# Cross-attention on one core: Wk loaded by row groups, two output tiles projected one batch later, the last tile's halves in two PSUM tiles

## The chip, the core and the metric

The kernel runs on 1 core of one Trainium2 chip. Its engines are TensorE (PE in the profile, with its weight loads as PEld), VectorE (DVE), ScalarE (ACT), GpSimd (POOL) and SyncE (SP), which does no arithmetic here and issues most of the DMA transfers. The metric is the device time of one execution in microseconds (us). Before the change the median of three runs was 953.03 us (952.38 to 954.02).

## What is computed

For each of 16 batches, with x of 100 rows by 640, a context of 718 rows by 384 (`enc`) and 4 more context rows (`ca`), in float32 throughout:

```python
query = x @ Wq;  keyt = enc @ Wk;  valt = enc @ Wv
hs = mha(query, keyt, valt)                       # 8 heads of 80
ca_q1 = einsum('btc,th->bch', ca, Wq_ca)[:, indices, :]
ca_hs1 = mha(ca_q1, x, x)
ca_q2 = ca_hs1 @ Wq;  ca_k2 = ca @ Wk_ca;  ca_v2 = ca @ Wv_ca
hs = hs + mha(ca_q2, ca_k2, ca_v2)
out = hs @ Wout + b_out + x
```

`mha` is softmax(q k^T / sqrt(80)) v for each head. The parts that matter for the change are the weight Wk, which is read once at the start, and the last line, the projection with Wout, whose rows are the 16 x 100 = 1600 rows of all batches.

## The kernel before

**Stages.** A startup part loads all weights and the first context, builds the values of batch 0 (`first_values`), folds Wk_ca with Wq (`k2_ps`, `m_ps`), transposes Wk on TensorE (`w_ps`, L1037) and makes the keys of batch 0 from it (`first_keys`, `kT_ps` L549), then the value projection of the 4 context rows (`va_ps`) and the queries of batches 0 and 1 (`q_ps` L525). After that a loop of 16 passes follows, one for each batch. In a pass PE makes scores (`s_ps` L604), small products of the second attention (`z_ps`, `y_ps`), the transpose of the previous batch's result (`hst_ps` L907), blocks of values and keys (`v_psA` to `v_psE` L425, `k_psA` to `k_psE` L456), the last chunk of the next batch's keys (`kT_ps`), perhaps a projection (`o_ps` L932), in odd passes the queries of the next two batches, and at last the attention sums (`a_ps` L1287). Up to the loop a scheduler orders the instructions of each engine; from `ctx.enter_context(tc.manual_schedule(...))` on they stand as written.

**Wk.** The host hands over Wk transposed: `wkt` has 640 rows (output columns of Wk) of 384. It is loaded into the space of `kT` as `wkt_sb`, five chunks of 128 partitions. `packed(w, c)` picks the rows of chunk c. For c below 4 these are 32 rows out of each of four groups of 160 rows (`RG` = 4, a group is two heads), so that group r lies on partitions 32r to 32r+31; chunk 4 holds the last 16 rows of each of the 8 heads. Each chunk is one transfer of 192 KB, issued by SP (L294), in program order. SP's queue has, in this order: pieces of the first context, `cat`, `wkca`, `wqt` (1600 KB), three more pieces of the context, `xT`, `ca`, the five pieces of `wkt`, five pieces of `wq`, `wvca`, and then `m_d`, which stores `m`. In the compiled program the transfers of SP and ACT take eight completion semaphores in turn, and a transfer waits, before it is issued, for the one that used its semaphore last.

The transposes of chunk c wait for chunk c's transfer alone; ACT copies each from PSUM into `wk_sb` or `wk4` (L1040), and `kT_ps` for a chunk needs the copy of this chunk only.

**The projection.** The 1600 rows are cut into tiles that don't follow the batches:

```python
OC = [(r, P) for r in range(0, B * S - P - 64, P)] + [(B * S - P - 64, 64), (B * S - P, P)]
```

These are eleven tiles of 128 rows, one of 64 and a last one of 128. A tile is projected when its last row's batch is done: `Last(b)` takes those whose end falls into batch b (`load`, L881), and pass b+1 calls its methods as `last`: `last.load()` loads the rows of x into `xn` on SP's queue and adds the bias on POOL (L892), `last.project()`, late in the pass, after the last keys and ahead of the queries and of `a_ps`, makes 10 matmul instructions into `o_ps` (two banks of 320 columns in one tile of two banks, `pair`), adds x on DVE (L951), and SP stores the rows (L952). Tiles end in batches 1, 2, 3, 5, 6, 7, 8, 10, 11, 12, 14, 14 and 15; none ends in 0, 4, 9 or 13. So tile 6 (rows 768 to 895, ends in batch 8) is projected in pass 9, tile 9 (rows 1152 to 1279, ends in batch 12) in pass 13. Passes 9 and 13 also have the queries; passes 10 and 14 have neither queries nor a projection. `hsT` and `xn` have two buffers each.

**The last tile.** Batch 15's tile is projected after the loop, in three calls of `project` for parts of its five chunks. Both halves (columns 0 to 319 and 320 to 639) lie in one two-bank tile; each half is added on DVE (L945) and stored by SP (L948) on its own. The pool `ps2`, which `pair` and `bank` draw from, has two tiles of two banks.

Of the kernel before, what the change touches and what calls it, by code (L numbers as in the profile page):

```python
# [10 lines left out]
ALU = mybir.AluOpType  # L11
# [3 lines left out]
B, S, H = 16, 100, 640  # L15
NH, D = 8, 80
CAD, T = 384, 4
SK = 722 - T
P = 128
HC = H // P  # L20
# [10 lines left out]


OC = [(r, P) for r in range(0, B * S - P - 64, P)] + [(B * S - P - 64, 64), (B * S - P, P)]
HT = NH * T

QC = [(0, 64), (64, S)]
# [10 lines left out]
for h in range(NH):  # L47
    lo = h * D
    while lo < (h + 1) * D:
        c = lo // P  # L50
        hi = min((h + 1) * D, (c + 1) * P)
        PIECES.append((h, c, lo - h * D, lo - c * P, hi - lo))
        lo = hi
# [15 lines left out]
RG = 4  # L69


def packed(w, c):

    if c < 4:
        lo = (c // 2) * D + 32 * (c % 2)
        return w.rearrange("(r k) n -> r k n", r=RG)[:, lo : lo + 32]
    return w.rearrange("(h k) n -> h k n", h=NH)[:, 64:]

# [44 lines left out]
def kernel(  # L125
# [18 lines left out]
    nc = tc.nc  # L144
# [14 lines left out]
    def pair(name):  # L159
        tile = ps2.tile([P, 2, 512], F32, tag="ps2", name=name)  # L160
        return tile

    def bank(name):
        return pair(name)[:, 0]
# [18 lines left out]
    def scores_tile(name):  # L183
        return main.tile([P, 2, ROWS], F32, tag="st", name=name, bufs=NP)

    def hs_tile(name):
        return main.tile([P, H], F32, tag="hs", name=name)

    def hsT_tile(name):
        return main.tile([P, HC, P], F32, tag="hsT", name=name, bufs=2)  # L190

    def xn_tile(name):
        return main.tile([P, H], F32, tag="xn", name=name, bufs=2)

    def vb_tile(name):
        return main.tile([P, T, H], F32, tag="vb", name=name)
# [46 lines left out]
    def in_order(dma):  # L243
        tc.keep_in_program_order(dma)
# [27 lines left out]
    for g in range(2):  # L272
        for c in range(CC):
            nc.scalar.dma_start(
                out=wv_sb[:, 2 * c + g],
                in_=wv[c * P : (c + 1) * P, g * (H // 2) : (g + 1) * (H // 2)],
# [9 lines left out]
    wkt_sb = kT.rearrange("p c u k -> p c (u k)")  # L286
# [3 lines left out]
    in_order(nc.sync.dma_start(out=xT, in_=xt[0:2].rearrange("b p c s -> p b c s")))  # L290
    ca_0 = small.tile([S, T, S], F32, tag="ca", name="ca_0", bufs=2)
    in_order(nc.sync.dma_start(out=ca_0, in_=cas[0].unsqueeze(0).to_broadcast([S, T, S])))
    for c in range(HC):
        in_order(nc.sync.dma_start(out=wkt_sb[:, c, :CAD], in_=packed(wkt, c)))  # L294
    halves = [t[:, u] for t in [scores_tile(f"wq_{i}") for i in range(NP)] for u in range(2)]
    room = halves.pop()
    wq_in = [t[:, :H] for t in halves]
# [16 lines left out]

    m2 = const.tile([P, HC, NG, HT], F32, name="m2")
    nc.gpsimd.memset(m2, 0.0)
    for h, c, r, s, k in PIECES:
        nc.gpsimd.dma_start(
            out=m2[s : s + k, c, GROUPS[c][1].index(-1), h * T : (h + 1) * T],
            in_=wqcat[h * D + r : h * D + r + k, :],  # L320
# [4 lines left out]
    for c in range(HC):  # L325
        first = c * P - HEADS[c][0] * D
        nc.gpsimd.affine_select(
            out=hmask[:, c], in_=hmask[:, c], compare_op=ALU.is_ge, fill=0.0,
# [3 lines left out]
            out=hmask[:, c], in_=hmask[:, c], compare_op=ALU.is_ge, fill=0.0,  # L332
# [6 lines left out]

    m_sb = [t[:, : B * HT] for t in (hs_tile("m_0"), xn_tile("m_1"), xn_tile("m_2"))]  # L340
    m_sb += [
        hsT_tile(f"m_{c}").rearrange("p c s -> p (c s)")[:, : B * HT] for c in range(3, HC)
    ]
    m_d = dram.tile([HC, P, B * HT], F32, name="m_d")

# [7 lines left out]
    for j in range(2):  # L353
        y = const.tile([S, NH, HT + 1], F32, name=f"y_{j}")
        nc.gpsimd.memset(y[:, :, HT:], 1.0)
        ys.append(y)
# [352 lines left out]
    class Second:  # L709
# [98 lines left out]
        def load(self):  # L808
            b = self.b
            self.vb = vb = vb_tile(f"vb_{b}")  # L810
            nc.gpsimd.dma_start(
                out=vb[:S],
                in_=va_d[b * T : (b + 1) * T, :].unsqueeze(0).to_broadcast([S, T, H]),
            )
# [58 lines left out]
    class Last:  # L873
# [7 lines left out]
        def load(self):  # L881

            self.xn = {}
            for r, (lo, n) in enumerate(OC):
                if not self.b * S < lo + n <= (self.b + 1) * S:
                    continue
                xn = self.xn[r] = spare[1] if r == len(OC) - 1 else xn_tile(f"xn_{r}")
                rows = x.rearrange("b s n -> (b s) n")[lo : lo + n]
                for at, cols in self.parts(n):
                    to = xn[at : at + n, : cols.stop - cols.start]  # L890
                    nc.sync.dma_start(out=to, in_=rows[:, cols])
                    nc.gpsimd.tensor_tensor(to, to, bias[at : at + n, cols], ALU.add)  # L892
# [7 lines left out]
        def transpose(self, chunks=[(0, HC)]):  # L900
# [4 lines left out]
            for c0, c1 in chunks:  # L905
                for c in range(c0, c1):
                    nc.tensor.transpose(  # L907
                        t_v[:, c], hs[:S, c * P : (c + 1) * P], ident[:S, :S]
                    )
                for r, (lo, n) in enumerate(OC):  # L910
                    first, end = max(lo, b * S), min(lo + n, (b + 1) * S)
                    if first >= end:
                        continue
                    if r not in hsTs:
                        hsTs[r] = (
                            spare[0].rearrange("p (c s) -> p c s", c=HC)
                            if r == len(OC) - 1
                            else hsT_tile(f"hsT_{r}")
# [6 lines left out]
        def project(self, chunks=range(HC)):  # L925
            for r, xn in self.xn.items():
                lo, n = OC[r]
                if chunks[0] == 0:
                    self.o_ps = pair(f"o_ps_{r}")
                o_ps = self.o_ps  # L930
                for c, k in [(c, k) for k in range(2) for c in chunks]:
                    nc.tensor.matmul(  # L932
                        o_ps[:n, k, : H // 2],
                        hsTs[r][:, c, :n],
                        wout_sb[:, c, k * (H // 2) : (k + 1) * (H // 2)],
                        start=(c == 0),
                        stop=(c == HC - 1),
                    )
                if chunks[-1] < HC - 1:
                    continue  # L940
                o_v = out.rearrange("b s n -> (b s) n")[lo : lo + n]
                if self.split:
                    for k in range(2):
                        cols = slice(k * (H // 2), (k + 1) * (H // 2))
                        nc.vector.tensor_tensor(  # L945
                            xn[:n, cols], o_ps[:n, k, : H // 2], xn[:n, cols], ALU.add
                        )
                        nc.sync.dma_start(out=o_v[:, cols], in_=xn[:n, cols])  # L948
                    continue
                both = xn[:n].rearrange("p (k d) -> p k d", k=2)  # L950
                nc.vector.tensor_tensor(both, o_ps[:n, :, : H // 2], both, ALU.add)  # L951
                nc.sync.dma_start(out=o_v, in_=xn[:n])  # L952

        def project_few(self, r):
            lo, n = OC[r]
            xn = self.xn.pop(r)
            o_ps = psumk(f"o_ps_{r}")
            for c in range(HC):
                for at, cols in self.parts(n):
                    nc.tensor.matmul(  # L960
                        o_ps[at : at + n, : H // 2],
                        hsTs[r][:, c, :n],
                        wout_sb[:, c, cols],
                        start=(c == 0),
                        stop=(c == HC - 1),
                    )
            nc.vector.tensor_tensor(
                xn[:, : H // 2], o_ps[:, : H // 2], xn[:, : H // 2], ALU.add
            )
            o_v = out.rearrange("b s n -> (b s) n")[lo : lo + n]  # L970
            for at, cols in self.parts(n):
                nc.sync.dma_start(out=o_v[:, cols], in_=xn[at : at + n, : H // 2])
# [26 lines left out]
    for n, heads in enumerate(HEADS):  # L999
        cols = len(heads) * B * T  # L1000
# [77 lines left out]
    for n in range(2):  # L1078
        nc.scalar.dma_start(
            out=va_d[:, n * (H // 2) : (n + 1) * (H // 2)],  # L1080
            in_=va[n * B * T : (n + 1) * B * T],
# [20 lines left out]
    for b in range(B):  # L1102
        p = b // 2
# [174 lines left out]
        for g in range(2):  # L1278
# [20 lines left out]
            cols = slice(4 * g * D, 4 * (g + 1) * D)  # L1299
# [65 lines left out]
```

## Time and profile before

| what | value |
|---|---|
| median of three runs | 953.03 us (952.38 to 954.02) |
| the profiled execution | 953.95 us |
| its span on the core | 952.2 us |
| mean granted clock of TensorE | 0.998 |
| DVE, ACT, POOL busy | 677.3, 362.1, 628.4 us |
| HBM traffic | 64 GB/s over the span |

The span runs from the first to the last instruction that the hardware profiler has on the core; 1.75 us of the execution lie outside it. "Busy" is the time in which an engine works on instructions; idle time before a group is put down to what released it. Of the largest groups on PE, `s_ps` has 3072 matmul rows of 32x100 and 768 of 32x200, `a_ps` 3072 rows, and `o_ps` 130 matmul instructions that show as 260 rows, because each float32 matmul stands as two rows in the trace. POOL's sums of context blocks (`enc`, L491) make up 101.6 + 32.8 us, in 180 instructions.

The startup up to the first scores takes 65.7 us. Lines of the stages below are given as L numbers of the kernel before.

### The profile page before, as it was taken

The numbers are of one execution on the slowest core, as the hardware profiler recorded it, in microseconds if no ns is written. First come the engines' busy times: TensorE is split into PE (matmuls) and PEld (weight loads), VectorE is DVE, ScalarE is ACT, GpSimd is POOL, SyncE is SP. The second block draws the span as 40 slices with busy tenths as digits, with TensorE's granted clock in tenths as the row PEclk, the third lists the DMA queues.
The fourth block names the chain that finished last, engine by engine and source line by source line (L and its number), as shares of the span: only waits on it lengthen the run. The fifth ranks groups of instructions, "written<-read, shape, count | busy, mean of one in ns | idle before, by whom it ended". The sixth has DMA issues, their size and how long they took to land.

```text
span 952.2 us, 25609 instructions
## 1 busy us (share of the span) xinstructions
PE 939.3 (99%) x11215; PEld 799.2 (84%) x11215; DVE 677.3 (71%) x1083; ACT 362.1 (38%) x598; POOL 628.4 (66%) x570
## 2 busy tenths in 40 slices
PE   9899999999999999999999999999999999999998
PEld 6898879879898888978789787898889888898866
DVE  1659795786928879496964959569793786928883
ACT  1234442444314344343524335243431444314341
POOL 4639979576846677496773958638694576845723
PEclk9999999999999999999999999999999999999999
DMA  8743014031130402204050040401204031120100
GB/s 253 221 142 98 3 44 136 2 95 37 50 102 1 115 2 80 59 1 129 1 149 3 6 125 1 136 3 46 71 17 135 2 100 31 47 84 1 59 8 29
DMA packets 45255, 62.48 MB, mean 66 GB/s; under 512 B 13336, under 2 KB 37208, under 8 KB 43544
## 3 DMA queue, kind: packets, MB, share of 16 engines
q1 hardware_dynamic: 41608, 42.97, 15.2%
q0 software_dynamic: 2512, 16.72, 6.0%
q8 instruction: 88, 1.44, 0.6%
q10 hardware_dynamic: 1024, 1.15, 0.4%
q14 instruction: 23, 0.19, 0.1%
HBM read 55.26 MB, written 5.57 MB: 64 GB/s over the span
## 4 chain that ended last, share of the span: by engine, by line
PE 94%; DMA 3%; DVE 1%; ACT 0%; issue 0%; SPq 0%; ACTq 0%; DVEq 0%
PE s_ps L604 12%; PE a_ps L1287 12%; PE v_psA L425 10%; PE v_psB L425 8%; PE k_psA L456 7%; PE kT_ps L549 7%; PE q_ps L525 7%; PE o_ps L932 7%; PE k_psB L456 6%; PE v_psC L425 3%; PE k_psC L456 3%; PE v_psD L425 2%; PE v_psE L425 2%; PE y_ps L730 2%; DMA kT<-in_wkt 1%; PE k_psE L456 1%
## 5 line engine op out<-in xcount | busy, mean ns | idle before, releaser
L765 POOL TENSOR_TENSOR e<-ca,g 100x800 f32<-100x800 f32 x64 | 99.4, 1564 | 135.0 <-DVE most L1136 120.9
L854 POOL TENSOR_TENSOR hs<-vb,p 100x640 f32<-100x640 f32 x64 | 105.0, 1650 | 45.9 <-DVE p L840 37.9
L861 POOL TENSOR_TENSOR hs<-hs,hs 100x640 f32<-100x640 f32 x48 | 115.1, 2397 | 3.8
L1287 PEld LDWEIGHTS a_ps<-vs,st 120*64 120x64 f32 (+3 forms) x3072 | 109.1, 125 | 7.3 <-issue 5.9
L1287 PE MATMUL a_ps<-vs,st 120*64 120x81 f32 (+3 forms) x3072 | 112.3, 234 | 1.6 <-ACT st L1132 1.0
L425 PE MATMUL v_psA<-wv_sb,enc 128*120 128x320 f32 x360 | 112.0, 434 | 0.0
L1124 DVE TENSOR_TENSOR st<-st,over 120x1600 f32<-120x1600 f32 x48 | 108.2, 2255 | 0.0
L491 POOL TENSOR_TENSOR enc<-enc 128x240 f32<-128x240 f32 x135 | 101.6, 766 | 7.1
L604 PE MATMUL s_ps<-qp,kT 32*120 32x100 f32 x3072 | 98.0, 263 | 0.8 <-issue 0.8
L621 ACT COPY st<-s_ps 120x800 f32<-120x800 f32 x64 | 49.7, 829 | 126.2 <-PE s_ps L604 126.2
L604 PEld LDWEIGHTS s_ps<-qp,kT 32*120 32x120 f32 x3072 | 95.1, 179 | 2.6 <-issue 1.2
L772 POOL TENSOR_TENSOR e<-e,e 100x800 f32<-100x800 f32 x48 | 92.2, 1922 | 3.8
L425 PE MATMUL v_psB<-wv_sb,enc 128*120 128x320 f32 x300 | 93.1, 433 | 0.0
L456 PE MATMUL k_psA<-enc,wk_sb 128*128 128x240 f32 x360 | 87.6, 366 | 0.0
L1298 DVE RECIPROCAL rs<-a_ps 100x4 f32<-100x4 f32 x32 | 5.8, 182 | 113.8 <-PE a_ps L1287 113.8
L425 PEld LDWEIGHTS v_psA<-wv_sb,enc 128*120 128x120 f32 x360 | 64.5, 183 | 23.0 <-issue 0.5
L1136 DVE TENSOR_TENSOR most<-most,st 120x800 f32<-120x800 f32 x64 | 66.4, 1038 | 22.8 <-ACT st L615 21.8
L1132 ACT ACTIVATE st<-st 120x1600 f32<-120x1600 f32 x48 | 73.8, 1538 | 23.1 <-DVE st L1124 23.1
L456 PEld LDWEIGHTS k_psA<-enc,wk_sb 128*128 128x128 f32 x360 | 68.3, 190 | 16.7
L491 POOL TENSOR_TENSOR enc<-enc,rest 128x240 f32<-128x240 f32 x45 | 32.8, 729 | 73.0 <-DMA rest<-in_enct 24.9
L425 PEld LDWEIGHTS v_psB<-wv_sb,enc 128*120 128x120 f32 x300 | 54.8, 183 | 22.1 <-DVE vs L396 0.4
L456 PE MATMUL k_psB<-enc,wk_sb 128*128 128x240 f32 x300 | 73.1, 366 | 0.0
(137 smaller groups left out, 1769.4 us busy)
## 6 DMA issues: line engine op xcount, KB each, us to landing
vb<-va_d POOLq DMA_DIRECT2D x16, 1000.0 KB, 7.8
enc<-in_enct SPq DMA_DIRECT2D x30, 240.0 KB
enc<-in_enct SPq DMA_DIRECT2D x15, 360.0 KB
xT<-in_xt SPq DMA_DIRECT2D x8, 500.0 KB
rest<-in_enct SPq DMA_DIRECT2D x31, 120.0 KB
xn<-in_x SPq DMA_DIRECT2D x11, 320.0 KB
out<-xn SPq DMA_DIRECT2D x11, 320.0 KB
ca<-in_cas SPq DMA_DIRECT2D x16, 156.2 KB
```

Source lines behind the costliest of these rows:

```text
L425: nc.tensor.matmul(at[0][j][:KN, : H // 2], a_form(self.enc, f)[:, j * KN : (j + 1) * KN], wv_sb[:, W_AT[f]], start=first, stop=last, skip ...
L456: nc.tensor.matmul(at[:, i * KT : (i + 1) * KT], wk_sb[:, W_AT[f], i], a_form(self.enc, f), start=(first and i == 0), stop=last, skip_grou ...
L491: nc.gpsimd.tensor_tensor(out, left, right, op)
L525: nc.tensor.matmul(q_ps[:, : 2 * S].rearrange("p (j s) -> p j s", j=2), wq_sb[:, c, n * P : (n + 1) * P], xT[:, :, c, :], start=(c == 0), ...
L604: nc.tensor.matmul(s_ps[r][:n, 256 * a + lo : 256 * a + hi], kT[rows, c, u, j * KN : (j + 1) * KN], rhs, start=(a == 0 and c == 0), stop=( ...
L765: first = nc.gpsimd.tensor_tensor(to, self.ca[:, t, :].unsqueeze(1).to_broadcast([S, NH, S]), g[:, :, t].unsqueeze(2).to_broadcast([S, NH, ...
L772: nc.gpsimd.tensor_tensor(e, e, to, ALU.add)
L854: first = nc.gpsimd.tensor_tensor(to, vb[:S, t, :].rearrange("p (h d) -> p h d", h=NH), p2[:, :, t].unsqueeze(2).to_broadcast([S, NH, D]), ...
L861: nc.gpsimd.tensor_tensor(sums, sums, to, ALU.add)
L1124: return nc.vector.tensor_tensor(st[i], st[i], top.over[:KN].unsqueeze(1).to_broadcast([KN, 2, ROWS]), ALU.subtract,)
L1132: nc.scalar.activation(st[i], st[i], AF.Exp, scale=SCALE)
L1287: nc.tensor.matmul(a_v[lo:hi, h % 4], st[i // 2][: KEYS[i], i % 2, h * S + lo : h * S + hi], block(i, h // 4)[: KEYS[i], h % 4], start=(i ...
```

## The change

Three edits. Wk's chunks 0 to 3 are loaded in eight transfers instead of four, each for one row group r and one of its two heads u: 32 partitions, two chunks at a time, 96 KB. Chunk 4 is loaded as before. Tiles are assigned to passes by `O_AFTER` in place of their end: a tile that ends in an even batch b goes to batch b+1 when no tile ends there. That holds for b = 8 and b = 12, so tile 6 is projected in pass 10 and tile 9 in pass 14; their loads and bias adds move along. The last tile's halves lie in two tiles of PSUM, each the first bank of a pair.

```diff
+ENDS = [(lo + n - 1) // S for lo, n in OC]
+O_AFTER = [b + 1 if b % 2 == 0 and b + 1 not in ENDS else b for b in ENDS]
...
-def packed(w, c):
-
-    if c < 4:
-        lo = (c // 2) * D + 32 * (c % 2)
-        return w.rearrange("(r k) n -> r k n", r=RG)[:, lo : lo + 32]
-    return w.rearrange("(h k) n -> h k n", h=NH)[:, 64:]
+def load_packed(load, to, w):
+
+    rows = w.rearrange("(r u k) n -> r u k n", r=RG, u=2)
+    for r, u in [(r, u) for r in range(RG) for u in range(2)]:
+        load(
+            out=to[32 * r : 32 * r + 32, 2 * u : 2 * u + 2],
+            in_=rows[r, u, :64].rearrange("(j p) n -> p j n", j=2),
+        )
+    load(out=to[:, 4], in_=w.rearrange("(h k) n -> h k n", h=NH)[:, 64:])
...
-    for c in range(HC):
-        in_order(nc.sync.dma_start(out=wkt_sb[:, c, :CAD], in_=packed(wkt, c)))
+    load_packed(
+        lambda **ends: in_order(nc.sync.dma_start(**ends)), wkt_sb[:, :, :CAD], wkt
+    )
...
             for r, (lo, n) in enumerate(OC):
-                if not self.b * S < lo + n <= (self.b + 1) * S:
+                if self.b != O_AFTER[r]:
                     continue
...
-                if chunks[0] == 0:
-                    self.o_ps = pair(f"o_ps_{r}")
+                if chunks[0] == 0 and self.split:
+                    self.o_ps = [bank(f"o_ps_{r}_{k}") for k in range(2)]
+                elif chunks[0] == 0:
+                    self.o_both = pair(f"o_ps_{r}")
+                    self.o_ps = [self.o_both[:, k] for k in range(2)]
...
-                        o_ps[:n, k, : H // 2],
+                        o_ps[k][:n, : H // 2],
...
-                            xn[:n, cols], o_ps[:n, k, : H // 2], xn[:n, cols], ALU.add
+                            xn[:n, cols], o_ps[k][:n, : H // 2], xn[:n, cols], ALU.add
...
-                nc.vector.tensor_tensor(both, o_ps[:n, :, : H // 2], both, ALU.add)
+                nc.vector.tensor_tensor(
+                    both, self.o_both[:n, :, : H // 2], both, ALU.add
+                )
```

Nothing else differs. In the compiled program the instructions of ACT keep their order; on PE and DVE the projections of the two tiles stand one pass later, on POOL and SP their bias adds, loads and stores. SP issues four transfers more. In the transposes of Wk on PE, those of chunks 0 and 1 now wait for the four transfers with u = 0, those of chunks 2 and 3 for the four with u = 1.

## The prediction

> **What bounds the kernel now.** I read the page first: the engine totals, then the 40 slices, then the chain that ended last.
>
> ```profile
> PE 939.3 (99%) x11215; PEld 799.2 (84%) x11215; DVE 677.3 (71%) x1083; ACT 362.1 (38%) x598; POOL 628.4 (66%) x570
> ...
> PE   9899999999999999999999999999999999999998
> ...
> PE 94%; DMA 3%; DVE 1%; ACT 0%; issue 0%; SPq 0%; ACTq 0%; DVEq 0%
> ```
>
> PE is busy for 939.3 of 952.2 us. No step of the change takes a matmul away, so all it can win is idle PE, slow PE and the tail behind the last matmul. The only slices under 9 are the second and the last. The list of PE's waits names the largest single one: the transposes of Wk, for the transfers into kT, 2.6 us, once. A table in steps of 1 us around it shows what that wait costs (columns: window, length, busy time and count of PE, PEld, DVE, ACT, POOL, granted PE clock, share of the 16 DMA engines, GB/s):
>
> ```profile
> 23.00:24.00 1.00, 1.00 (x9) 1.00 (x8) 0.53 (x3) 0.00 (x0) 0.00 (x0) 1.00 0.27 100
> ...
> 31.00:32.00 1.00, 0.82 (x6) 0.58 (x6) 0.26 (x1) 0.47 (x2) 0.75 (x3) 1.00 0.83 224
> 32.00:33.00 1.00, 0.00 (x0) 0.00 (x0) 0.00 (x0) 0.67 (x3) 1.00 (x1) 1.00 0.73 138
> 33.00:34.00 1.00, 0.00 (x0) 0.00 (x0) 0.00 (x0) 0.00 (x0) 1.00 (x2) 1.00 0.79 201
> 34.00:35.00 1.00, 0.60 (x3) 0.63 (x4) 0.00 (x0) 0.00 (x0) 0.92 (x2) 0.53 1.08 376
> 35.00:36.00 1.00, 1.00 (x7) 0.80 (x6) 0.00 (x0) 0.26 (x1) 1.00 (x1) 0.50 1.02 368
> 36.00:37.00 1.00, 1.00 (x5) 0.94 (x5) 0.75 (x2) 0.94 (x3) 0.92 (x2) 0.50 1.02 393
> 37.00:38.00 1.00, 1.00 (x6) 0.90 (x5) 1.00 (x2) 0.14 (x1) 1.00 (x1) 0.77 1.04 383
> ```
>
> See two things: PE stands still from 31.82 to 34.40, and then runs 3.5 us at half clock. And at 23 us, with Wk the only load under way, 0.27 of 16 engines, about four, move 100 GB/s; at 14 to 16 us the same table gives 406.
>
> **Part 1, the load of Wk.** SP issues its transfers in order, and each waits for the one eight places earlier in the program. So later issues show when pieces of Wk landed (timeline of SP, and of PE):
>
> ```profile
> 28.72 0.33 SPq L299 DMA_DIRECT2D wq<-in_wq  x1
> 31.47 0.38 SPq L300 DMA_DIRECT2D wvca<-in_wvca  x1
> 34.35 0.33 SPq L1026 DMA_DIRECT2D m_d<-m  x1
> ...
> 34.40 2.01 PE L1037 MATMUL w_ps<-ident,kT 128*128 128x128 f32 x8 [2.58 <-DMA kT<-in_wkt]
> ```
>
> These wait for the second, third and fourth piece: 192 KB every 2.8 us. PE starts 0.05 us after the fourth; the fifth frees SP at 35.68.
>
> Why four engines? [...] Old pieces are 4x32x384 into 128x384: 4 engines, as the row at 23 us has it. New ones are 32x2x384 on both sides: 16. [...]
>
> When do the new pieces land? The first goes at 12.24. The second waits for wkca (the present second piece, 14.98, has that wait), the third to sixth for wqt and enc (from 20.13, about 0.5 us apart). The seventh and eighth wait for xT and ca; the present second and third wq transfers, which do so too, are out by 24.34 and 25.59. The ninth waits for the first. All are issued by about 26.1, and 960 KB at 300 to 400 GB/s is 2.5 to 3.3 us, which runs from about 23. Last landing: about 28, at the latest 26.1 + 2.8 = 28.9. The transposes begin at 30.19. So **the wait goes**, although a chunk is now whole only with its fourth row group, the seventh piece for chunks 0 and 1.
>
> What is late next? The first six transposes end at 31.82 as before (m and y_ps precede them). Two of chunk 3 follow, to 32.05. Chunk 2 takes the PSUM bank of y_ps, which ACT copies out until 31.91 + 0.38 = 32.29. Seven more at 0.11 to 0.15 us end at 33.1 to 33.4. kT_ps then starts at 33.2 instead of 36.42: **3.2 us**. Its first eight matmuls take 2.14 us now (36.42 to 38.56), later ones 0.2025 each, so 1.62: another **0.5 us** of clock. [...] The row shows half clock after 2.58 us, and the mean clock of 0.998 is 1.7 us lost in the whole run, all here. I take 3.7, ends 2.4 (a new wait) and 4.3 (2.58 + 1.7).
>
> Is it given back? wq and wvca leave SP earlier than now. DVE's copies of wq (36.25 to 45.2) start near 31.7, beside POOL's e products, and q_ps needs them only at 57.1 - 3.7. The POOL sums for batch 1 start at 62.78, when enc lands; that load waits for PE's va_ps, so it moves along, but wout and xT, held by POOL, don't, and may delay it by 1 us. POOL idles 1.18 us after the sums, so I cost that at nothing; without this cover it costs up to 1 us. The stalls of batches 0 and 1 (a_ps 1.0, hst_ps 1.2) hang on DVE and ACT, which hang on PE: they move along and stay.
>
> **Part 2, two tiles one batch later.** Tile 6 moves from pass 9 to pass 10, tile 9 from 13 to 14: per tile 20 o_ps rows (5.4 us of PE), one DVE add (0.82), one POOL bias add (about 0.8 to 1.6), one load and one store on SP. PE's sum stays. Passes 9 and 13 keep q_ps (8.5 us) between kT_ps and a_ps, as pass 5 has it now; passes 10 and 14 have nothing there now. The chain behind pass 10:
>
> ```profile
> 665.84 6.90 PE a_ps L1287 x191
> 672.73 0.40 PE s_ps L604 x8
> 673.13 0.80 issue
> 673.93 7.29 PE s_ps L604 x224
> ...
> 681.53 0.18 issue
> ...
> 683.84 1.10 PE v_psA L425 x4
> ```
>
> From s_ps to v_psA is 11.11 us; nearly every other pass has 9.52 (624.33 to 633.85). **1.6 us** are lost, and PE waits for nothing that the profile names. My reading is late instructions: a_ps and s_ps are hundreds of short ones, and here they come without a pause while DMA is 0.91 to 1.02 busy (664 to 672). Passes with 5.4 us of o_ps ahead of the same burst don't show it. With o_ps in pass 10, a_ps starts when the burst is over. I take 1.6; ends 1.8 (pass 14 loses 0.2) and a loss of 0.6 (a gap like the one of 0.57 in batch 1 appears elsewhere).
>
> The rest is covered. In pass 10 the bias add stands on POOL before the products that wait 2.2 us for DVE. The DVE add comes while PE runs 6.9 us of a_ps. Of SP: loads of tiles 10 and 11 and of spare now queue behind the store of tile 9. In the present clock pass 14's o_ps would end at 894.3 (894.31 is a_ps's start now; pass 13 gives back what pass 14 takes), so the store goes near 895.5 in place of 838.46. Tile 11 also needs it landed; loads then land by about 901, POOL's bias adds (3.3 us for these tiles now) end by 905, and the DVE add that needs them comes at 916.02. Slack 11 us; cost nothing, one for one beyond it.
>
> **Part 3, the last tile's halves.** Now both halves share a tile, and DVE waits for all of it:
>
> ```profile
> 943.96 4.35 PE o_ps L932 x16
> ...
> 948.33 0.49 DVE spare L945
> ...
> 948.90 0.84 SPq L948 DMA_DIRECT2D out<-spare  x2
> ```
>
> Five of these eight matmul instructions (two rows each, 0.54 us) finish half 0, at 946.7; its add and store lie beside the last three. Half 1 is added at 948.33 and not 0.4 later, and its store, second of 0.84 us, is issued 0.4 to 0.5 earlier with no other on the queue: **0.5 us**, ends 0.2 and 0.9. The second tile takes the pair that tile 10's add left at 935.5, long before.
>
> **The sum.** 3.7 + 1.6 + 0.5 = 5.8. The profiled execution took 953.95 (span 952.2, 1.75 around it): 948.15. It stands 0.9 above the median of 953.03, inside the runs' 952.38 to 954.02; from the median the sum gives 947.2. I put the forecast between, at **947.6**.
>
> **Rivals.**
> - The gap of pass 10 is bad luck of one place, and stays or moves. For: the trace has it once. Against: eleven covered passes are free of it. Startup and tail alone: 4.2, so 949.2. Chance 0.2.
> - Another wait takes the place: enc's load behind wout, then POOL's 11.2 us of sums in batch 0, eats 2.5 us of the startup's gain. Against: the POOL slack above. 950.1. Chance 0.1.
> - The change doesn't do what it says: Wk lands as late as now, because SP's waits and not engines hold it. Then parts 2 and 3 alone, 951.5. Against: only four engines move at 23 us. Chance 0.05.
> - Slower: the engines of a piece are counted from its dimension of 2, not of 32. By the same rule two engines then carry 256 rows each where four carry 128 each in 13.57 us (20.69 to 34.26 in the chain): 27 us, landing at 48, and kT_ps 13 us late; 953.5 + 13 - 2.1, about 964. It decides once the last piece lands over 2.1 us later than the present 35.6. Against: the program issues 32x2x384 with 32 outermost. Chance 0.04.
>
> The forecast has 0.61. A measurement of this kernel tells about 0.2%, 1.9 us, from no change. Faster by more: forecast, the first two rivals and part of the third, 0.91; same 0.05; slower 0.04. The range adds up low ends (4.3 + 1.8 + 0.9 from the median, and runs that differ by 0.5) and goes up to the second rival: 945.6 to 950.5.
>
> **What would show it.** Right: no wait of w_ps for kT, kT_ps near 33.2, clock 1.00 from 30 to 40 us, DMA share near 1 at 24 us; s_ps to v_psA 9.52 us in batch 11; the first spare add near the end of half 0. Wrong: clock below 1 there, "issue" gaps at other passes, a wait of POOL's enc sums that grows, or o_ps of pass 14 followed by a late L967 add.

## The result, and the profile after

The changed kernel takes **946.35 us** in the median of six runs (945.60 to 946.49); the kernel before took 953.28 us beside it (six runs, 952.38 to 954.02). The ratio is 0.9924, with a 95% interval of 0.9915 to 0.9934, so 6.9 us less (6.3 to 8.1). The profiled execution took 945.6 us, its span 943.9.

The page of the changed kernel: engine totals, PE's 40 slices, and the shares of the chain that ended last.

```profile
PE 935.4 (99%) x11215; PEld 796.8 (84%) x11215; DVE 680.7 (72%) x1083; ACT 361.8 (38%) x598; POOL 626.0 (66%) x570
...
PE   9999999999999999999999999999999999999998
...
PE 95%; DVE 3%; ACT 1%; DMA 0%; issue 0%; POOL 0%; ACTq 0%; DVEq 0%
```

PE has the same 11215 rows, 3.9 us less of busy time, and no slice under 9 at the start any more. DMA has 0% of the chain in place of 3%.

The startup, in windows of 1 us (columns as in the prediction: length, busy time and count of PE, PEld, DVE, ACT, POOL, granted clock of PE, share of the 16 DMA engines, GB/s):

```profile
22.00:23.00 1.00, 1.00 (x10) 1.00 (x9) 0.21 (x2) 0.00 (x0) 0.00 (x0) 1.00 1.01 195
23.00:24.00 1.00, 1.00 (x10) 1.00 (x9) 0.62 (x1) 0.00 (x0) 0.29 (x1) 1.00 0.65 139
24.00:25.00 1.00, 1.00 (x10) 1.00 (x10) 0.69 (x1) 0.00 (x0) 0.00 (x0) 1.00 0.23 63
...
31.00:32.00 1.00, 1.00 (x10) 0.97 (x8) 1.00 (x1) 1.00 (x3) 1.00 (x1) 1.00 0.93 317
32.00:33.00 1.00, 1.00 (x7) 0.94 (x6) 1.00 (x2) 0.50 (x2) 1.00 (x2) 1.00 1.02 369
33.00:34.00 1.00, 1.00 (x7) 0.94 (x6) 1.00 (x3) 0.00 (x0) 0.92 (x2) 1.00 1.01 320
34.00:35.00 1.00, 1.00 (x7) 0.94 (x6) 1.00 (x1) 0.56 (x1) 1.00 (x1) 1.00 0.97 369
```

From 31 us on PE is busy and at full clock, where it stood still and then ran at half clock before. But at 24 us the DMA share is 0.23 and not near 1: the engines are full at 22 us and three quarters idle two microseconds later. The timeline of SP's queue and of PE, in the same kernel:

```profile
12.14 13.89 SPq L302 DMA_DIRECT2D kT<-in_wkt  x9
26.08 2.35 SPq L308 DMA_DIRECT2D wq<-in_wq  x5
...
29.83 1.82 PE L1051 MATMUL w_ps<-ident,kT 128*128 128x128 f32 x13
31.50 1.38 PE L558 MATMUL kT_ps<-enc,wk_sb 128*128 128x240 f32 x6
```

Nine transfers of Wk are issued by 26.03, and the transposes of Wk don't wait for them. Wk's rows can be told from all others in the traces' DMA records, as packets of 1536 bytes, 640 of them. In the changed kernel 358 have started by 24 us, at up to 118 in 1 us (181 GB/s). The last three transfers are issued from 23.81 on, and the last row is in at 28.72. In the kernel before, 127 have started by 24 us and the last row is in at 34.81. From its traces:

```profile
23.67 5.37 SPq L299 DMA_DIRECT2D wq<-in_wq  x5
...
28.00:29.00 1.00, 1.00 (x10) 1.00 (x9) 0.69 (x1) 0.00 (x0) 0.03 (x1) 1.00 1.09 274
```

Here wq shares the engines with Wk. Its first rows move at 25.05, when 210 rows of Wk have started, and in each microsecond from 26 to 32 only 33 to 48 rows of Wk start, where it was 65 at 23 us. In both kernels wq stands behind Wk in SP's queue, but it takes SP longer to get nine transfers out than five (13.89 us against 11.39). In the changed kernel wq is issued from 26.08 and moves from 27.40, when 533 rows of Wk have started. So the change did two things at once: it gave Wk's pieces more engines, and it put wq off.

The chain behind pass 10 (start, length, what):

```profile
654.26 5.38 PE o_ps L944 x20
659.64 6.90 PE a_ps L1301 x191
666.54 7.28 PE s_ps L613 x240
673.82 0.68 PE z_ps L801 x56
...
676.07 1.10 PE v_psA L434 x4
```

`o_ps` of tile 6 now stands ahead of `a_ps`. No piece is called "issue", and from `s_ps` to `v_psA` it is 9.53 us, against 11.11.

The tail, in the timeline of all engines:

```profile
935.77 4.50 PE L944 MATMUL o_ps<-wout_sb,spare 128*128 128x320 f32 x16
...
938.69 0.49 DVE L957 TENSOR_TENSOR spare<-o_ps,spare 128x320 f32<-128x320 f32 x1 [3.29 <-PE o_ps L944]
939.26 1.90 SPq L960 DMA_DIRECT2D out<-spare  x2
940.31 0.49 DVE L957 TENSOR_TENSOR spare<-o_ps,spare 128x320 f32<-128x320 f32 x1 [1.12 <-PE o_ps L944]
```

The first add lies beside `o_ps`, and only the second is left behind its end at 940.27.

Where the 8.3 us between the two profiled spans lie, by the same marks in both traces:

| stretch | before | after | difference |
|---|---|---|---|
| start to the first `k_ps` | 20.22 | 18.83 | -1.39 |
| `k_ps` to `kT_ps` | 16.20 | 12.67 | -3.53 |
| `kT_ps` to `q_ps` | 20.61 | 20.09 | -0.52 |
| behind pass 10, `s_ps` to `v_psA` | 11.11 | 9.53 | -1.58 |
| pauses in batch 1 and pass 12 | | | -1.00 |
| end of the last `o_ps` to the end | 3.90 | 3.63 | -0.28 |

The first row is not of the change. `k_ps` starts before anything that the change touches is needed, and in the eleven profiles here, all with the same early loads, it starts at 18.3 to 20.2. Nor are the pauses of the fifth row shown to be: in batch 1 a kernel with all three parts has one of 0.30 us (the last experiment), and the kernel with the tiles alone has none. Without these two rows the pair differs by 5.9 us.

### The profile page after: what moved, and what is told of

Same layout as the page of the kernel before. It is cut to its first block, busy times and chain, and to the rows that moved or that the text cites. A ratio compares the mean times of both kernels' runs of the same rounds, so it can differ in the third digit from the quotient of the medians.

```text
span 943.9 us, 25613 instructions
## 1 busy us (share of the span) xinstructions
PE 935.4 (99%) x11215; PEld 796.8 (84%) x11215; DVE 680.7 (72%) x1083; ACT 361.8 (38%) x598; POOL 626.0 (66%) x570
## 3 DMA queue, kind: packets, MB, share of 16 engines
q8 instruction: 88, 1.44, 0.7%
## 4 chain that ended last, share of the span: by engine, by line
PE 95%; DVE 3%; ACT 1%; DMA 0%; issue 0%; POOL 0%; ACTq 0%; DVEq 0%
PE s_ps L613 12%; PE a_ps L1301 12%; PE v_psA L434 10%; PE v_psB L434 9%; PE kT_ps L558 7%; PE k_psA L465 7%; PE q_ps L534 7%; PE o_ps L944 7%; PE k_psB L465 6%; PE v_psC L434 3%; PE k_psC L465 2%; PE v_psD L434 2%; PE v_psE L434 2%; PE y_ps L739 2%; PE v_ps L375 1%; PE k_psE L465 1%
## 5 line engine op out<-in xcount | busy, mean ns | idle before, releaser
L500 POOL TENSOR_TENSOR enc<-enc 128x240 f32<-128x240 f32 x135 | 99.2, 749 | 7.1
L500 POOL TENSOR_TENSOR enc<-enc,rest 128x240 f32<-128x240 f32 x45 | 33.9, 752 | 68.3 <-DMA rest<-in_enct 36.0
```

The costliest lines, as they stand in the source:

```text
L500: nc.gpsimd.tensor_tensor(out, left, right, op)
```

## Experiments: one part at a time

Three kernels have one part of the change each, and a fourth has Wk's load cut so that about two DMA engines carry it (2.2 by the DMA share). They ran beside 29 runs of the kernel before (median 953.02).

**Wk's load alone.** The kernel before with the new load:

```diff
-    for c in range(HC):
-        in_order(nc.sync.dma_start(out=wkt_sb[:, c, :CAD], in_=packed(wkt, c)))
+    load_packed(
+        lambda **ends: in_order(nc.sync.dma_start(**ends)), wkt_sb[:, :, :CAD], wkt
+    )
```

> Only Wk's load by row groups. If startup is worth what the two profiles show from k_ps on (3.5 us of wait, 0.5 us of clock), kT_ps starts 12.7 us after k_ps, where it was 16.2, the clock stays at 1.00 from 30 to 40 us, and the time falls by 4.0 to 4.8 us (0.7 more if the gap of 0.57 us in batch 1 goes with it), the gap behind pass 10 staying. If part of the gain was luck of one execution, the time falls by 3 us or less.

Measured: 948.26 us (947.74 to 948.85), ratio 0.9948 (0.9935 to 0.9960), so **-4.8 us**, more than the forecast's 3.7. `k_ps` to `kT_ps` is 12.66 us and `kT_ps` to `q_ps` 20.09, as in the full change. From the last `o_ps` to the end it is 4.2 us, 0.25 more than before; the last experiment shows why. The pause of pass 10 is still there, in its chain:

```profile
666.22 0.39 PE s_ps L609 x7
666.61 1.03 issue
667.64 7.14 PE s_ps L609 x233
```

**Tiles 6 and 9 alone.** The kernel before with `O_AFTER`:

```diff
-                if not self.b * S < lo + n <= (self.b + 1) * S:
+                if self.b != O_AFTER[r]:
```

> Only the two tiles moved. If the gap behind pass 10 is in every execution of the kernel before and goes because of the move, s_ps to v_psA behind pass 10 takes 9.52 us and the time falls by 1.5 to 1.9 us. If the gap was luck of one profile, the time changes by less than 0.5 us. The startup has its wait of about 2.6 us and its half clock as before in both.

Measured: 951.03 us (950.13 to 953.56), ratio 0.9983 (0.9976 to 0.9991), **-2.0 us**. The pause is gone (9.53 us from `s_ps` to `v_psA`, against 11.11). This execution also shows that the startup's cost is not a fixed number. Its windows around the wait for Wk:

```profile
33.00:34.00 1.00, 0.00 (x0) 0.00 (x0) 0.00 (x0) 0.00 (x0) 1.00 (x2) 0.97 0.42 151
34.00:35.00 1.00, 0.01 (x1) 0.04 (x1) 0.00 (x0) 0.00 (x0) 0.92 (x2) 0.50 0.80 195
...
39.00:40.00 1.00, 1.00 (x4) 0.87 (x3) 1.00 (x1) 0.00 (x0) 1.00 (x1) 0.50 0.93 347
40.00:41.00 1.00, 1.00 (x4) 0.85 (x4) 1.00 (x3) 0.00 (x0) 0.92 (x2) 0.62 0.79 266
```

PE waits 3.16 us here, and the clock is halved from 33.9 to about 40.8, 6.8 us in place of 3.4. `k_ps` to `kT_ps` is 16.71, `kT_ps` to `q_ps` 21.97: 5.9 us above the row groups' 12.66 and 20.09, where the trace that I predicted from has 4.05.

**The halves alone.**

```diff
-                    self.o_ps = pair(f"o_ps_{r}")
+                    self.o_ps = [bank(f"o_ps_{r}_{k}") for k in range(2)]
...
-                            xn[:n, cols], o_ps[:n, k, : H // 2], xn[:n, cols], ALU.add
+                            xn[:n, cols], o_ps[k][:n, : H // 2], xn[:n, cols], ALU.add
```

> Only the last tile's halves in two PSUM tiles. From the last o_ps row to the end of the span 3.9 us before. If the second store's earlier issue counts in full, 3.4 us, and the time falls by 0.5. If the two profiles' difference of 0.3 is all that the edit can give, 3.6. With the transfers numbered as before, the store's place in the last list of waits is the same as before, which tells these two apart. The time can't settle this; the profile can.

Measured: 952.23 us (949.64 to 954.17), ratio 0.9989 (0.9979 to 0.9999), -0.8 us. The profile is sharper than the time: from the last `o_ps` to the end of the span it is 3.4 us against 3.9, the full 0.5. In the whole change it is 3.6.

**Two engines per piece.** Eight transfers of 96 KB as in the change, but each takes two row groups of one chunk, so the slowest dimension (the outermost of the transfer's source) is 2 and not 32:

```diff
+    rows = w.rearrange("(r k) n -> r k n", r=RG)
+    for c, g in [(c, g) for c in range(4) for g in range(2)]:
...
+            out=to[64 * g : 64 * g + 64, c],
+            in_=rows[2 * g : 2 * g + 2, lo : lo + 32],
```

> Wk alone, in as many transfers and as many bytes in each as the changed kernel (eight of 96 KB, then chunk 4), but each of 64 partitions from a source of 2x32x384. If the number of engines decides, two engines carry each, the DMA share falls to near 2 of 16, kT_ps starts up to 13 us later than before, and the time rises by 8 to 13 us. If the number of transfers or SP's order of waits decides, it is as fast as Wk by row groups: down by 4 to 5 us.

Measured: 959.96 us (959.14 to 960.10), ratio 1.0069 (1.0055 to 1.0082), **6.9 us slower** than before (5.2 to 7.8), a little less than the 8 to 13 us expected. Its windows of 2 us:

```profile
24.00:26.00 2.00, 2.00 (x17) 2.00 (x17) 1.29 (x2) 0.00 (x0) 0.35 (x1) 1.00 0.14 50
```

and the timeline of its PE:

```profile
39.82 2.15 PE L1029 MATMUL w_ps<-ident,kT 128*128 128x128 f32 x9 [9.40 <-DMA kT<-in_wkt]
41.77 1.86 PE L541 MATMUL kT_ps<-enc,wk_sb 128*128 128x240 f32 x6
```

At 24 us Wk alone is under way, with 0.14 of 16 engines, 2.2, and 50 GB/s; the kernel before had 0.27 and 100 at 23 us, with Wk alone. PE then waits 9.40 us for it, and `kT_ps` starts 23.28 us after `k_ps`, 7.1 later than before. The number of transfers, their size and their place in SP's queue are those of the change, and wq comes late here too (issued from 30.39). What differs is which rows a piece holds and how many engines are at work on Wk, and the kernel lands on the other side of the one before. So with 2.2 engines Wk is late even when it has them to itself.

## Experiments: what the parts consist of

These ran beside 27 runs of the kernel before (median 953.71), the last one beside 11 others (953.37).

**The price of a small transfer.** Wk's load alone, in sixteen pieces of 48 KB:

```diff
-    for r, u in [(r, u) for r in range(RG) for u in range(2)]:
+    for c, r in [(c, r) for c in range(4) for r in range(RG)]:
         load(
-            out=to[32 * r : 32 * r + 32, 2 * u : 2 * u + 2],
-            in_=rows[r, u, :64].rearrange("(j p) n -> p j n", j=2),
+            out=to[32 * r : 32 * r + 32, c],
+            in_=rows[r, c // 2, 32 * (c % 2) : 32 * (c % 2) + 32],
```

> Wk's load alone, in sixteen transfers of 48 KB (32 rows by one chunk, 16 engines each) and the ninth piece, instead of eight of 96 KB; compare with Wk's load alone by row groups (948.3 us, 4.8 below the kernel before). Theory (the number of engines decides, and a transfer more costs SP's issue, about 0.43 us, and not a latency of its own): eight more issues delay the last landing by 0 to 3.4 us, which the slack of 0 to 2 us before the transposes of Wk hides in part; the time is 0 to 2 us more than Wk's load alone, so still 2.5 to 4.8 us below before. [...]

Measured: 950.64 us (949.84 to 951.07), ratio 0.9963 (0.9950 to 0.9975), -3.1 us in the medians. So eight more transfers give back part of the gain and not all of it. The timeline of PE shows a wait again, and the windows why:

```profile
24.00:25.00 1.00, 1.00 (x10) 1.00 (x9) 0.69 (x1) 0.00 (x0) 0.02 (x1) 1.00 0.32 75
25.00:26.00 1.00, 1.00 (x10) 1.00 (x9) 0.47 (x1) 0.00 (x0) 0.32 (x1) 1.00 0.44 108
```

```profile
32.55 0.52 PE L1028 MATMUL w_ps<-ident,kT 128*128 128x128 f32 x3 [1.26 <-DMA kT<-in_wkt]
```

At shares of 0.32 and 0.44 the engines stand idle more than half of the time: 108 GB/s is 48 KB each 0.46 us, about the 0.43 us that one issue took on SP (`wvca` at 31.15, same run). The last of Wk's issues ends at 28.72, 2.7 us later than the changed kernel's, and `k_ps` to `kT_ps` is 14.12 us, 1.46 more. For eight more transfers that is 0.18 us each, less than one issue, so they don't queue up with a latency of their own each. The wait of 1.26 us leaves the clock at 1.00.

One more thing can be read from this run. Until wq's first rows move, Wk runs at 57 rows a us here, and at the same 57 in the kernel before. But here wq comes at 29.92, when 526 of the 640 rows have started. The kernel gains 2.1 us from `k_ps` to `kT_ps` all the same. That points at wq's later place as a good part of the gain.

**The clock's share.** The kernel before, with matmuls of no use on PE while it waits for Wk:

```diff
+        for _ in range(10 if c == 3 else 0):
+            nc.tensor.matmul(
+                w_ps[:, CC * P : CC * P + P], idle, idle, start=True, stop=True
+            )
```

> The kernel before, with ten additional matmuls of idle by idle into unused columns of the bank that chunk 3's transposes use, so that nine of them stand on PE between the transposes of chunk 2 and those of chunk 3, while PE waits for Wk. The load of Wk is as before, so it lands as before. Theory (part of the startup's gain is the clock, which halves while PE is idle): kT_ps starts at about the same distance after k_ps as before (16.2 us, 0.5 less at most), its first eight matmuls take about 1.6 instead of 2.1 us, kT_ps to q_ps takes 20.1 to 20.3 instead of 20.6 to 22.0 us, and the time is 0.5 to 1.9 us less than before. Rival (the clock halves whatever stands on PE at that place, or the dummies are over long before Wk lands): half clock remains in the slices after 34 us and the time stays within 0.3 us.

Measured: 953.02 us (950.80 to 955.03), ratio 0.9992 (0.9984 to 1.0000). The time alone would not settle it. The windows do:

```profile
33.00:34.00 1.00, 0.19 (x3) 0.07 (x2) 0.00 (x0) 0.48 (x1) 0.93 (x1) 1.00 1.03 351
34.00:35.00 1.00, 1.00 (x7) 0.96 (x8) 0.57 (x1) 0.48 (x1) 0.94 (x1) 1.00 1.02 391
35.00:36.00 1.00, 1.00 (x7) 0.94 (x6) 1.00 (x3) 0.00 (x0) 0.98 (x1) 1.00 1.12 420
```

Wk lands as late as before (`k_ps` to `kT_ps` 15.90 us), and yet the clock is 1.00 and `kT_ps` to `q_ps` is 20.09, as in the changed kernel. PE's longest wait for Wk is 0.81 us here, against 2.58 in the kernel before. So the half clock comes from PE's idling, and in this pair of profiles it was a cost of 0.5 us of its own. Of the 22 runs, twelve have a mean clock of 1.000; their mean is 952.4. The chain of the profiled one holds a pause of 1.43 us in pass 10, the one that the next experiment is about; it stands in `a_ps` here:

```profile
663.43 6.55 PE a_ps L1291 x180
669.99 1.43 issue
```

Seven runs have a mean clock of 0.998 and a mean of 954.3 us, so the clock was halved somewhere in them; where, no profile shows.

**The pause behind pass 10.** The kernel before, where only the 1000 KB transfer into `vb` is issued later in pass 10:

```diff
-            second.load()
+            if b != 10:
+                second.load()
...
+        if b == 10:
+            second.load()
```

> The kernel before, with one edit: in pass 10 alone the transfer into vb (1000 KB, issued on POOL) is started after keys and enc_sums, so that the burst of transfers no longer lies under a_ps and s_ps. Nothing else of the change is in it. Theory (the pause of PE behind pass 10 comes from instructions that are fetched late because the burst holds the 16 DMA engines): s_ps to the next group falls from 11.0 us to 9.4 to 10.0, no row of 'issue' above 0.3 us stands there, and the time is 0.5 to 1.6 us less than before. Rival (bad luck of one place, or a wait that the profile does not name): s_ps to the next group stays at 10.9 to 11.0 us and the time stays. If vb itself comes too late, PE waits by name for DVE or DMA in pass 10 and the time is longer by that wait.

Measured: 951.47 us (950.27 to 951.77), ratio 0.9968 (0.9956 to 0.9980): 2.2 us in the medians, above the 1.6 expected. The chain in pass 10 has no pause:

```profile
665.01 6.90 PE a_ps L1290 x191
671.91 7.28 PE s_ps L604 x240
679.19 0.68 PE z_ps L792 x56
```

The interval is 1.9 to 4.2 us, so there is more gain here than the pause alone; what the rest is stays open.

That the pause depends on the burst is shown by this run. What PE may be waiting for shows when PE's rows (15682 matmuls and weight loads and 127 semaphore and drain rows up to the pause in the kernel before) are counted from the start of the program, and the transfers of q8 ("instruction" on the page: 88 transfers of 16 KB, 1.44 MB) are laid beside them:

| kernel | rows of PE up to the pause | pause begins | a 16 KB transfer of q8 | PE goes on |
|---|---|---|---|---|
| before | 15809 | 673.13 | 671.50 to 672.63 | 673.93 |
| Wk's load alone | 15809 | 666.61 | 665.25 to 666.34 | 667.64 |
| dummy matmuls | 15809 | 669.99 | 668.49 to 669.76 | 671.42 |
| tile 6 put back | 15809 | 668.59 | 668.11 to 669.24 | 670.83 |

The halves alone, the sixteen pieces and the two engines per piece have 15809 too. The kernel with the dummy matmuls has 20 matmuls more ahead of this place, and its pause stands 19 matmuls earlier in the program, in `a_ps` and not in `s_ps`. So the pause belongs to a place in PE's stream of instructions, and not to an operation. After the startup, seventeen pauses of PE over 0.12 us in the eleven profiles have no named cause, these seven among them. Each stands a whole number of 256 rows from this place, and in each PE goes on 1.3 to 1.7 us after a transfer of q8 has ended. My reading is that PE has run out of instructions there and waits for those that the transfer brings; no record names the wait.

With the burst that transfer comes later. In the seven profiles with the pause in pass 10 it starts 5.1 to 6.9 us after `a_ps` began; in the four without, 2.9 to 4.4 (5.7 in the kernel before, 4.4 with `vb` late).

POOL is no second witness. It stands still for 4.07 us before 672.37, with no wait that the profile names, but also for 5.78 us before 331.15 and for 3.68 us before 784.62, where PE has no pause. It does so behind its own issue of the transfer into `vb`, and what holds it there is not shown.

**Tile 6 put back.** The changed kernel, with tile 6 alone in its old pass:

```diff
-O_AFTER = [b + 1 if b % 2 == 0 and b + 1 not in ENDS else b for b in ENDS]
+O_AFTER = [
+    b + 1 if b % 2 == 0 and b + 1 not in ENDS and b > 8 else b for b in ENDS
+]
```

> The changed kernel with tile 6 alone put back into pass 9, so that pass 10 has no o_ps again ahead of a_ps; tile 9 stays in pass 14, the load of Wk and the halves stay. Theory (o_ps in pass 10 keeps the short instructions of a_ps and s_ps out of the burst of transfers there, and nothing else of part 2 counts much): a pause of PE of 0.8 to 1.4 us that the profile calls 'issue' is back in pass 10, inside s_ps or a_ps, the pass is 1.3 to 1.6 us longer from the start of a_ps to the group behind s_ps, and the time is 1 to 1.8 us more than the changed kernel's 946.35 us, about 947.4 to 948.2. Rival (the pause is a matter of the startup's or the burst's time, which are other here than before): no pause in pass 10, and the time within 0.5 us of the changed kernel's.

Measured: 948.02 us (947.20 to 952.48), ratio 0.9940 (0.9919 to 0.9962): 1.7 us above the changed kernel's median, and in the forecast stretch. All seven runs are above all six of the changed kernel. The profiled execution was the longest of the seven, and shows what the pause can do:

```profile
668.00:670.00 2.00, 0.59 (x13) 0.33 (x9) 1.17 (x3) 0.00 (x0) 0.00 (x0) 1.00 0.59 154
670.00:672.00 2.00, 1.17 (x40) 1.17 (x40) 0.00 (x0) 0.00 (x0) 1.60 (x3) 1.00 0.10 26
672.00:674.00 2.00, 2.00 (x49) 2.00 (x44) 0.00 (x0) 0.00 (x0) 1.84 (x4) 0.57 0.00 0
674.00:676.00 2.00, 2.00 (x51) 2.00 (x44) 0.28 (x1) 1.55 (x2) 1.93 (x3) 0.58 0.04 8
676.00:678.00 2.00, 2.00 (x80) 2.00 (x76) 0.78 (x1) 0.67 (x2) 1.97 (x2) 1.00 0.00 0
```

The pause took 2.24 us this time, and 1.4 us after PE had resumed the clock was halved until about 675.7: 49 rows in 2 us where 80 belong. From `s_ps` to `v_psA` it was 13.65 us, 4.1 more than 9.53.

**The end of SP's list.** After its last transfer SP waits for the eight completion semaphores in a fixed order, 0.063 us apart. In the changed kernel the last store's stands second, and the rest of the list comes behind its landing. The changed kernel with the last tile's input in five transfers, so that the last store takes another semaphore:

```diff
+                    for c in range(HC if r == len(OC) - 1 else 0):
+                        part = slice(c * P, (c + 1) * P)
+                        nc.sync.dma_start(out=to[:, part], in_=rows[:, part])
```

> The changed kernel with all three parts, and the last tile's input (spare, in_x) loaded in five transfers of 128 columns instead of one of 640, so that four more transfers stand on SP ahead of the last stores. Each completion is counted on one of eight semaphores in turn, and SP ends the kernel by waiting for all eight in a fixed order; the last store's then comes sixth instead of second. Theory: from the last o_ps to the end of the span falls from 3.6 to 3.4 us or less, everything ahead of it stays, and the time is 0.2 to 0.3 us less than the changed kernel's 946.35, which is at the edge of what can be measured. Rival (the order of that list is no cost, the tail lost its gain elsewhere): 3.6 us stay.

Measured: from the last `o_ps` to the end 3.36 us against 3.63, with the last landing 1.04 instead of 1.29 us ahead of the end. The time is 946.87 us (945.20 to 947.71), ratio 0.9921 (0.9909 to 0.9933), which can't be told from the changed kernel's 0.9924. The reading fits, and so does Wk's load alone: it has four transfers more on SP and no other change in the tail, its last store has the same early place, and its tail is 0.25 us longer than before. The gain is too small to be worth the transfers.

## Why the prediction was right, and which term was too small

The forecast of 947.6 us was 1.25 above the median, inside its range, and its likeliest case is what happened: the wait, the pause and part of the tail went. The road to the first was not the one forecast.

- **Startup, the wait: right that it goes, in part by another road.** Counting the engines by a piece's slowest dimension was the author's assumption. The number came out as taken: the DMA share gives 2.2, 4.3 and 16 of them (0.14, 0.27 and 1.01, the last at 22 us in the changed kernel, where the packets of Wk alone hold 14.7) for slowest dimensions of 2, 4 and 32; the runs show it for these three alone. The rate did not. The sum has 960 KB at 300 to 400 GB/s, from about 23 us, and its sign was a share near 1 at 24 us. Wk ran from 20.0 us, at 181 GB/s in its best row of the table, and at 24 us the share was 0.23. The last landing, 28.72 against "about 28, at the latest 28.9", came out because the earlier start and the lower rate cancel; that is luck. Why full engines move so little of Wk, when they moved 406 GB/s at 14 to 16 us, is not shown.
- **A rival that the prediction did not name: wq.** In the kernel before, wq takes part of the engines from 25.05 on. By an estimate from that trace, the 430 rows then left would have taken 6.6 us more at the 65 rows a us of 23 us, to 31.7, and PE fell idle at 31.82. So four engines with wq held back might have lost most of the wait too. Two engines with wq held back were not enough. Old pieces with wq issued later were not run, so how the gain divides between engines and order stays open.
- **The named rivals.** That SP's waits and not the engines hold Wk is refuted as the whole cause by the two-engine kernel, whose transfers have the same order and number. Eight transfers of 96 KB in place of four of 192 KB are 4.8 us faster, and the sixteen show what a further cut costs: an issue every 0.46 us, once that is the slowest part.
- **Startup, size: too small.** The term that was off is the "**0.5 us** of clock", and with it the 3.7. In the profile pair the sum was 4.05 (3.53 + 0.52), inside its ends; `kT_ps` came at 31.50, which with the 1.39 us of the earlier start is 32.9 against the 33.2 of the forecast. But alone, by medians, this part is worth 4.8 us (3.8 to 6.2). I took wait and half clock from one execution. By the same marks that loss, against the row groups alone, is 4.05 us in the kernel before, 4.35 with the halves alone, 4.48 with `vb` late and 5.94 with the tiles alone: mean 4.7. The half clock's part of these is 0.5, 0.7, 0.9 and 1.9. My bound of 1.7 us, the whole clock deficit of that one run, was exceeded in another. The runs tell how common that is: of 67 of the kernel before, 47 have a mean clock of 0.998, 19 have 0.995 to 0.997 and one has 1.000.
- **What was given back: nothing, as forecast.** POOL's sums for batch 1 start at 57.44 in place of 62.78, its slack behind them is 1.18 us as before, and the loads of the last tiles follow the store of tile 9 at 887.29 and have their bias by 896.9, ahead of the adds.
- **Pass 10: right, and the traces fit its cause.** "Late instructions" is what the place of the pause points at: the 15809th row, with PE going on 1.3 to 1.7 us behind the end of a 16 KB transfer of q8. No record names it. 1.58 us in the profile pair, 2.0 alone (0.9 to 2.3), 1.7 missing when tile 6 is put back. The rival "bad luck of one place" falls: a pause of 0.8 to 2.2 us stood in pass 10 in every profile without `o_ps` there and with `vb` in its old place (six kernels besides the one before), and in none of the four others. What the sum didn't have is that the pause can halve the clock as well. How often it does is open: one profile shows it.
- **Tail: right alone, 0.28 in the whole.** The 0.5 was measured with the halves alone. Together with the other parts, the four more transfers of Wk on SP moved the last store to an early place in the list of semaphores, and 0.25 us went back. No term of the forecast was for the semaphore that the last store would take.
- **The slower rival** had the right place and sign: engines from a dimension of 2 give 6.9 us slower. Its 964 was 4 us too high: it doubled the 13.57 us from issue to last landing, in which wq slowed Wk. At the measured 50 GB/s the 960 KB take 19 to 20 us, and PE had Wk at 39.8 and not at 48.

The three parts alone add up to 4.8 + 2.0 + 0.8 = 7.6 us, the whole gives 6.9 (6.3 to 8.1): they add up within what can be measured.

## What to carry to other kernels

Count the DMA engines of a load from the share in a window where the load runs alone, and lay its slowest dimension beside it (here 2.2, 4.3 and 16 engines for 2, 4 and 32); cut it otherwise until the engines are all in, and no finer, since each further piece costs the queue an issue (0.46 us here). See too what stands behind it in the queue, and would share its engines before it is in. Price a wait of TensorE with the clock that it loses afterwards (0.5 to 1.9 us here), and take that from several executions. Where PE pauses and the profile says "issue", count its rows up to the pause in several profiles. If the count is the same although the program ahead differs, late instructions are a likely cause: look at what the DMA engines do at that moment, and put long matmuls there or move the burst (1.6 us less from `s_ps` to `v_psA` here).

## What the hardware did that I had not expected

- The half clock has no fixed price. In the startup it came 2.1 to 3.0 us after PE fell idle (34.06 against 31.82 in the kernel before, 32.49 against 30.42 with two engines per piece) and lasted 3.4 us, 6.8 with the tiles alone and 10.2 with two engines. With `vb` late it came when PE had been working again for 0.45 us; in pass 10, with tile 6 put back, 3.7 us after PE fell idle and 1.4 us after it went on. Idling of 0.8 to 1.4 us left the clock alone; 2.2 us (tile 6 put back) did not. The lengths of 6.8 and 10.2 us are two and three times 3.4; what sets them is not shown.
- PE stood still for 0.8 to 2.2 us at the same 15809th row in seven profiles, with no cause that the profile names, and did not when the burst was moved. The 256 rows between the places of such pauses, and the 16 KB transfers of q8 that end 1.3 to 1.7 us before PE goes on, fit late instructions; that PE waits for them is my reading. It is rare: 88 such transfers go with at most three pauses over 0.12 us in any of these profiles.
- The place of the last store in the list of semaphores at the end of this kernel is worth 0.25 us.
